# The paired mix products of a recurrent layer: a 32-column product of one of the two issued by itself ahead of the rest

## The chip, the core and the metric

The kernel runs on one core of a Trainium2 chip. The metric is the time of one execution on the device in microseconds (us). Three executions of the kernel before took 1084.72, 1081.46 and 1083.66 us; their median is 1083.66 us. A further execution was recorded by the hardware profiler, and all profile rows below are from that one.

A core has five engines, each with an instruction queue of its own that runs in order: PE (matrix products, with weight loads listed apart as PEld), DVE (vector), ACT (scalar functions), POOL (a second vector engine), and SP (which here only issues DMAs). Products land in PSUM, which has eight banks of 128 x 512 float32 values. DVE or ACT must read a bank out before it can be used again.

## The reference, cut to what matters

Four layers follow each other on an input `x` of 32 sequences, 64 positions, 256 features: a small attention layer (L0), two transformer layers with self-attention, cross-attention and an MLP (L1, L2), and a recurrent layer (L3). The change is in L3, whose head is this:

```python
xn = _ln(x, ln1_w, ln1_b)
sx = _token_shift(xn, state[:, i1])
xxx = jnp.tanh((xn + sx * maa_x) @ maa_w1).reshape(b, l, 5, 1, EXTRA_MAA)
xxx = jnp.matmul(xxx, maa_w2).reshape(b, l, 5, E)
x5 = xn[:, :, None] + sx[:, :, None] * (maa_stack + xxx)
...
k = (x5[:, :, 0] @ Wk.T).reshape(b, l, H, S)
v = (x5[:, :, 2] @ Wv.T).reshape(b, l, H, S)
```

So there are five mixes `x5[:, :, m]`, m = 0 to 4, each the product of a 32-wide piece of `xxx` with a 32 x 256 matrix, and each is then the input of one projection: 0 of the keys, 1 of the decay, 2 of the values, 3 of the receptance, 4 of the gate. After the projections a scan runs along the 64 positions, then come a group norm, an output projection and a feed-forward block. All in float32.

## The kernel before

**Tiling.** The 2048 rows of `x` (32 sequences times 64 positions) stay on the chip. The recurrent layer works through them in eight steps, n = 0 to 7, of four sequences (256 rows) each. `recurrent(n, ...)` returns three lists of pieces for a step: `first` (norm, mixes, projections, decay, gate), `second` (spreading the values by DMA, the scan, reading it with the receptance, the group norm, the output projection) and `third` (the feed-forward block). Data lie transposed: 256 features as two halves (c = 0, 1) of 128 partitions, 256 rows along the free dimension.

**The order of the work.** Each piece has a due time, and `emit` traces all pieces in the order of these times. Step n begins about one unit after step n - 1. Worked out from the parameters in lines 9 to 15 and the weights in lines 775 to 777, the norm of step n is due at n - 0.2, `mix(2, 3)` at n + 0.59, `mix(0, 1)` at n + 0.89 and `mix(4)` at n + 1.39; so the norm of step n + 1, due at n + 0.8, stands between the two paired mixes of step n. The pieces of the MLP of L2 that are left over (`late`) are interleaved with the steps in the same way. The final order within each engine's queue is not this one: a planner goes through the traced instructions with a simulated clock, and at each moment gives an engine the ready instruction that was traced earliest. An instruction that is the first to write a tile is ready only when one of the buffers of the tile's tag is free in that simulation. `tc.high_priority()` puts instructions ahead of all others that are ready, and `tc.issue_after(i)` keeps them behind `i` in their queue.

**PSUM.** The eight banks are shared out by tag (line 92): two each for `mm`, `sc` and `tp`, one each for `pc` and `pd`. In the recurrent layer `sc` has two kinds of users: the norm at the head of a step, `norm("x", ...)` in line 775, which takes one bank for its transposes (`pln_r`, line 163) and one for the token shift (`pst_r`, line 170), and the mixes (`px5_...`, which the profile lists as `px_r`).

**The mixes, lines 676 to 692.** `mix(*ms)` takes a bank for each mix in `ms` and lists four products for a pair, two for `mix(4)`: the stationary operand is a 32 x 128 piece of the matrix, the moving operand 32 x 256 of `ta` (or `tb` for m = 4), and the output one half c of the bank. Mix m uses partitions 32(m mod 4) to 32(m mod 4) + 31 of both operands, so the two mixes of a pair use different row groups of PE's array. The list runs c = 0: m = 3, m = 2; c = 1: m = 3, m = 2 (or 1, 0, 1, 0). `at_once` (lines 124 to 129) issues the first of them at its normal priority and the other three behind it with high priority. In the profile each float32 product is two weight loads and two matmul passes, so a pair of mixes shows as eight `MATMUL px_r` entries.

Then line 689 computes `(bank + maa_stack) * sx` on DVE, in two halves for each mix, which frees the bank, and line 692 adds `xn` on POOL. The projections `vals` (pv_r), `recept` (pr_r), `keys` (pk_r), `gate` (pg_r) and the decay (pdc_r, pw_r) follow, all on PE. DVE also runs the long operations of `second`: products with keys and receptance (line 782) and the scan (line 797), which read and write `vb_r`.

Of the kernel before, what the change touches and what calls it, by code (L numbers as in the profile page):

```python
# [23 lines left out]
P = 128  # L24
# [7 lines left out]
XM = 32  # L32
# [48 lines left out]
def tile_xattn_stack(ctx: ExitStack, tc: tile.TileContext, a: dict, out: bass.AP):  # L81
# [31 lines left out]
    def vec(name, i=0):  # L113
        c = VEC[name] + i
        return vecs[:, c : c + 1]
# [8 lines left out]
    def at_once(matmuls):  # L124

        first = matmuls[0]()
        with tc.issue_after(first.ins), tc.high_priority():
            for m in matmuls[1:]:
                m()

    def mm(ps, sta, mov, start=True, stop=True):
        return lambda: nc.tensor.matmul(ps, sta, mov, start=start, stop=stop)  # L132
# [467 lines left out]
    RB, RR = GB // 2, GR // 2  # L600

    def recurrent(n, pool, c3):
# [3 lines left out]
        st = {}  # L606
# [5 lines left out]
        def both(name, tag="mm"):  # L612

            return bank(name, tag).rearrange("p (c t) -> p c t", c=2)

        def tile_(name, bufs=2, shape=None, p=pool, tag=None):
            return p.tile(shape or [P, 2, RR], FP, tag=tag or name, name=f"{name}_{t}", bufs=bufs)
# [28 lines left out]
        def sx_(key, c):  # L646
            return st["d" + key][:, c].rearrange("p b t -> p (b t)")
# [28 lines left out]
        def mix(*ms):  # L676

            banks, mms = {m: both(f"px5_{t}_{m}", "sc") for m in ms}, []

            for c in range(2):  # L680
                for m in reversed(ms):
                    lw, rt = (c3["mw2a"], st["ta"]) if m < 4 else (c3["mw2b"], st["tb"])
                    part = slice((m % 4) * XM, (m % 4 + 1) * XM)
                    mms.append(mm(banks[m][:, c], lw[part, c * P : (c + 1) * P], rt[part, :RR]))
            at_once(mms)
            for m in ms:
                d = st["x5", m] = tile_(f"x5_{m}", tag="x5", bufs=3)
                for c in range(2):
                    nc.vector.scalar_tensor_tensor(  # L689
                        d[:, c], banks[m][:, c], vec("L3_maa_stack", 2 * m + c), sx_("x", c), ALU.add, ALU.mult  # L690
                    )
                nc.gpsimd.tensor_tensor(d, d, st["x"], ALU.add)  # L692
# [81 lines left out]

        first = [(0.5, lambda: norm("x", "L3_ln1_w", "L3_ln1_b", t, 1)), (0.0, first_mix), (1.2, maa)]
        first += [(0.85, lambda: mix(2, 3)), (1.7, vals), (0.85, lambda: mix(0, 1)), (1.7, recept), (1.7, keys)]
        first += [(0.85, lambda: mix(4)), (0.5, decay_a), (0.85, decay_b), (0.85, own_term), (1.7, gate)]


# [117 lines left out]
    wts, c3 = {}, {}  # L897
# [342 lines left out]
```

## Time and profile before

| what | value |
|---|---|
| three timed executions, median | 1083.66 us (1081.46 to 1084.72) |
| the profiled execution, its own time | 1080.68 us |
| its span, first to last instruction | 1078.9 us |
| PE busy | 983.6 us, 91% of the span, 10764 matmul passes |
| PEld busy | 787.8 us, 73% |
| DVE busy | 806.2 us, 75% |
| ACT busy | 549.2 us, 51% |
| POOL busy | 532.2 us, 49% |
| mean granted PE clock | 0.962 of full |

The span is the time from the first to the last instruction; the execution's own time is 1080.68 - 1078.9 = 1.78 us more than that. The busy time of an engine is the union of its instructions; matmuls overlap in a pipeline, so a full PE column does not mean that PE does as much as it could. A row of the timeline gives the start, the length, the engine, the line, the operation, output<-inputs, shapes and count, and in brackets how long the engine sat idle before it and what ended that. "L132" is the helper `mm`, through which the mixes and the over-keys sums go; the names `px_r` and `pa_r` tell them apart. The chain of waits goes back from the last instruction to whatever released it, so its rows say which engine's work set the end at each moment.

### The profile page before, as it was taken

What the parts mean: (1) busy time and instruction counts of PE and PEld (TensorE: products, weight loads), DVE (VectorE), ACT (ScalarE), POOL (GpSimd) and SP (SyncE); (2) the same over time, 40 slices, a digit from 0 to 9 for tenths busy, and PEclk for the clock granted to TensorE, in tenths of its full rate; (3) what the DMA queues carried; (4) which work ended last, traced back from release to release, by engine and by line L of the source; (5) the groups of instructions that cost most, each with busy time, mean ns of one, the idle gap of its engine ahead of it and who ended that gap; (6) DMA issues with size and microseconds to landing.
All of it is one profiled execution on the core that took longest, in us unless ns stands there. A gap on an engine that the chain in (4) does not pass through costs nothing.

```text
span 1078.9 us, 26319 instructions
## 1 busy us (share of the span) xinstructions
PE 983.6 (91%) x10764; PEld 787.8 (73%) x10764; DVE 806.2 (75%) x1513; ACT 549.2 (51%) x1271; POOL 532.2 (49%) x552
## 2 busy tenths in 40 slices
PE   8998999899989999989989999898989898988966
PEld 4886776667778989877767778787768677765645
DVE  5864688878877654777787887647887987999983
ACT  4743653554456644864454555454436464453334
POOL 4343766767657344756577665442434434153200
PEclk9999998999999999989899999999889999998889
DMA  9300111111100100140111101112122121332400
GB/s 301 105 21 21 23 45 32 38 25 27 26 22 7 40 1 21 46 138 22 41 39 28 26 21 32 31 36 66 41 70 60 50 61 40 95 76 69 98 11 29
DMA packets 45947, 53.39 MB, mean 49 GB/s; under 512 B 16146, under 2 KB 40068, under 8 KB 43780
## 3 DMA queue, kind: packets, MB, share of 16 engines
q1 hardware_dynamic: 40292, 49.60, 17.1%
q10 hardware_dynamic: 5536, 2.12, 0.8%
q8 instruction: 85, 1.39, 0.5%
q14 instruction: 34, 0.28, 0.1%
HBM read 38.83 MB, written 4.21 MB: 40 GB/s over the span
## 4 chain that ended last, share of the span: by engine, by line
PE 43%; DVE 32%; ACT 8%; POOL 8%; issue 4%; DMA 3%; SPq 0%; ACTq 0%; POOLq 0%; DVEq 0%
DVE vb_r L797 6%; PE pf_L1m L187 4%; PE pf_L2m L187 3%; DVE vb_r L782 3%; PE pfo_L1m L187 3%; POOL s_L2c L463 2%; DVE x L198 2%; POOL s_L1c L463 2%; PE pr L312 2%; PE pfo_L2m L187 2%; PE pwo_r L843 1%; PE px_r L132 1%; PE pq_L1c L187 1%; DVE s_L1c L458 1%; POOL s_L1s L463 1%
## 5 line engine op out<-in xcount | busy, mean ns | idle before, releaser
L692 POOL TENSOR_TENSOR x_r<-x_r,xn_r 128x512 f32<-128x512 f32 x40 | 63.6, 1604 | 113.7 <-DVE x_r L689 111.8
L797 DVE TENSOR_TENSOR_SCAN vb_r<-wsh,vb_r 128x512 f32<-128x512 f32 x64 | 77.6, 1276 | 5.6 <-ACT wsh L696 4.1
L463 POOL TENSOR_TENSOR s_L1s<-s_L1s,n 128x512 f32<-128x512 f32 x32 | 43.0, 1356 | 39.9 <-DVE s_L1s L458 39.2
L187 PE MATMUL pf_L2m<-lnT_L2m,w_L 128*128 128x256 f32 x384 | 57.8, 303 | 1.7 <-ACT vbd L430 0.7
L187 PEld LDWEIGHTS pf_L2m<-lnT_L2m,w_L 128*128 128x128 f32 x384 | 51.8, 202 | 7.6 <-issue 2.5
L187 PE MATMUL pfo_L2m<-w_L,hT_L2m 128*128 128x256 f32 x384 | 55.2, 291 | 1.5 <-DVE hT_L2m L581 1.5
L463 POOL TENSOR_TENSOR s_L2s<-s_L2s,n 128x512 f32<-128x512 f32 x32 | 43.0, 1360 | 26.9 <-DVE s_L2s L458 26.3
L187 PE MATMUL pfo_L1m<-w_L,hT_L1m 128*128 128x256 f32 x384 | 54.5, 288 | 1.6 <-POOL hT_L1m L580 0.8
L187 PE MATMUL pf_L1m<-lnT_L1m,w_L 128*128 128x256 f32 x384 | 51.9, 288 | 3.9 <-ACT hf_L1m L577 1.2
L463 POOL TENSOR_TENSOR s_L2c<-s_L2c,n_L2c 128x512 f32<-128x512 f32 x32 | 41.6, 1320 | 27.6 <-DVE s_L2c L458 26.7
L463 POOL TENSOR_TENSOR s_L1c<-s_L1c,n_L1c 128x512 f32<-128x512 f32 x32 | 41.3, 1309 | 25.8 <-DVE s_L1c L458 24.8
L187 PEld LDWEIGHTS pf_L1m<-lnT_L1m,w_L 128*128 128x128 f32 x384 | 47.5, 191 | 7.2 <-ACT hf_L1m L577 2.1
L187 PEld LDWEIGHTS pfo_L2m<-w_L,hT_L2m 128*128 128x128 f32 x384 | 48.7, 190 | 5.2 <-issue 2.7
L187 PEld LDWEIGHTS pfo_L1m<-w_L,hT_L1m 128*128 128x128 f32 x384 | 49.3, 191 | 3.4 <-POOL hT_L1m L580 1.0
L580 POOL TENSOR_SCALAR hT_L1m<-hf_L1m 128x512 fp32r<-128x512 f32 x32 | 21.8, 682 | 55.4 <-ACT hf_L1m L577 53.5
L577 ACT ACTIVATE hf_L1m<-pf_L1m,b_L 128x256 f32<-128x256 f32 x64 | 26.6, 471 | 42.3 <-PE pf_L1m L187 39.9
L581 DVE TENSOR_TENSOR hT_L1m<-hf_L1m,hT_L1m 128x512 fp32r<-128x512 f32 x32 | 25.3, 791 | 30.1 <-POOL hT_L1m L580 30.1
L581 DVE TENSOR_TENSOR hT_L2m<-hf_L2m,hT_L2m 128x512 fp32r<-128x512 f32 x32 | 24.7, 772 | 26.7 <-POOL hT_L2m L580 26.6
L580 POOL TENSOR_SCALAR hT_L2m<-hf_L2m 128x512 fp32r<-128x512 f32 x32 | 22.2, 694 | 40.1 <-ACT hf_L2m L577 39.8
L577 ACT ACTIVATE hf_L2m<-pf_L2m,b_L 128x256 f32<-128x256 f32 x64 | 26.6, 472 | 28.5 <-PE pf_L2m L187 23.0
L782 DVE TENSOR_TENSOR vb_r<-vb_r,ksh 128x2048 f32<-128x2048 f32 x16 | 38.3, 2409 | 2.7 <-DMA vb_r<-vd_r 2.7
L282 ACT ACTIVATE att<-pe,nmx 128x256 f32<-128x256 f32 x64 | 29.5, 476 | 19.3 <-DVE nmx L280 17.2
(388 smaller groups left out, 3062.1 us busy)
## 6 DMA issues: line engine op xcount, KB each, us to landing
vb_r<-vd_r SPq DMA_DIRECT2D x16, 1024.0 KB
raw_w_L<-in_L_w_dram SPq DMA_DIRECT2D x4, 1024.0 KB
y<-in_y_dram SPq DMA_DIRECT2D x8, 256.0 KB
x<-in_x_dram SPq DMA_DIRECT2D x8, 256.0 KB
ctxT_L1c<-in_yT_dram SPq DMA_DIRECT2D x4, 512.0 KB
kbd<-kT_L1s SPq DMA_DIRECT2D x64, 32.0 KB
kbd<-kT_L1c SPq DMA_DIRECT2D x64, 32.0 KB
kbd<-kT_L2s SPq DMA_DIRECT2D x64, 32.0 KB
```

The costliest lines, as they stand in the source:

```text
L132: return lambda: nc.tensor.matmul(ps, sta, mov, start=start, stop=stop)
L187: nc.tensor.matmul(ps, sta[x], mov[y], start=(at == 0), stop=(at == n - 1))
L198: nc.vector.tensor_tensor(xs, xs, ps, ALU.add)
L282: nc.scalar.activation(att[:, 2 * h + c, :], pe[:, c, :], AF.Exp, bias=nmx[:, h, c : c + 1], accum_out=rs[:, h, c : c + 1],)
L312: nc.tensor.matmul(pr[:, m, h, :], att[:, 2 * h + c, m * P : (m + 1) * P], xvT[:, c, h, :], start=(c == 0), stop=(c == 1),)
L463: nc.gpsimd.tensor_tensor(s[:, r], s[:, r], n(j).unsqueeze(1).broadcast_to([P, 8, S]), ALU.add)
L577: nc.scalar.activation(raw[:, i], ps[:, i], AF.Gelu_apprx_tanh, bias=w()["b1"][:, 2 * f2 + i : 2 * f2 + i + 1])
L580: nc.gpsimd.tensor_scalar(h[:, 0], raw, 1.0, 0.0, ALU.mult, ALU.add)
L581: nc.vector.tensor_tensor(h[:, 1], raw, h[:, 0], ALU.subtract)
L692: nc.gpsimd.tensor_tensor(d, d, st["x"], ALU.add)
L782: nc.vector.tensor_tensor(v, v, x.unsqueeze(1).broadcast_to([P, 4, 2 * RR]), ALU.mult)
L797: nc.vector.tensor_tensor_scan(v[:, d], flat(st["wsh"]), v[:, d], 0.0, ALU.mult, ALU.add)
```

## The change

For a pair of mixes, one more product is issued ahead of the four: half c = 0 of the pair's first mix (`ms[0]`: m = 2 or m = 0) for the first 32 of its 256 columns (`few = XM = 32`). It is issued at normal priority and is not part of the list given to `at_once`. It is the first to write that mix's bank. The list then holds the same four products in the same order, except that half 0 of `ms[0]` covers columns 32 to 255. For `mix(4)`, `few` is 0 and nothing changes. The products themselves are moved into a helper `add`.

```diff
@@ -677,11 +677,19 @@
             banks, mms = {m: both(f"px5_{t}_{m}", "sc") for m in ms}, []
 
+            def add(m, c, cols):
+                lw, rt = (c3["mw2a"], st["ta"]) if m < 4 else (c3["mw2b"], st["tb"])
+                part = slice((m % 4) * XM, (m % 4 + 1) * XM)
+                mms.append(mm(banks[m][:, c, cols], lw[part, c * P : (c + 1) * P], rt[part, cols]))
+
+
+            few = XM if len(ms) > 1 else 0
+            if few:
+                add(ms[0], 0, slice(0, few))
+                mms.pop()()
             for c in range(2):
                 for m in reversed(ms):
-                    lw, rt = (c3["mw2a"], st["ta"]) if m < 4 else (c3["mw2b"], st["tb"])
-                    part = slice((m % 4) * XM, (m % 4 + 1) * XM)
-                    mms.append(mm(banks[m][:, c], lw[part, c * P : (c + 1) * P], rt[part, :RR]))
+                    add(m, c, slice(few if c == 0 and m == ms[0] else 0, RR))
             at_once(mms)
```

## The prediction

> **What bounds the kernel now.** I begin with the page: the span, the busy times, and the chain of waits by engine.
>
> ```profile
> span 1078.9 us, 26319 instructions
> ...
> PE 983.6 (91%) x10764; PEld 787.8 (73%) x10764; DVE 806.2 (75%) x1513; ACT 549.2 (51%) x1271; POOL 532.2 (49%) x552
> ...
> PE 43%; DVE 32%; ACT 8%; POOL 8%; issue 4%; DMA 3%; SPq 0%; ACTq 0%; POOLq 0%; DVEq 0%
> ```
>
> PE is the busiest engine, but it holds only 43% of the chain and DVE holds 32%. The changed pieces run only in the last 366 us (first `px_r` at 713 us), so I read that stage next, as busy time in five stretches; the columns are the stretch, its length, and busy time (instructions) of PE, PEld, DVE, ACT, POOL, then PE clock, DMA share and GB/s.
>
> ```profile
> 700.00:780.00 80.00, 74.70 (x540) 63.09 (x539) 53.86 (x88) 40.50 (x85) 31.71 (x40) 0.94 0.20 48
> 780.00:860.00 80.00, 71.39 (x455) 56.20 (x456) 67.52 (x99) 36.64 (x72) 30.99 (x26) 0.94 0.25 60
> 860.00:940.00 80.00, 73.44 (x484) 59.87 (x483) 65.60 (x96) 42.12 (x86) 25.27 (x27) 0.98 0.22 54
> 940.00:1020.00 80.00, 72.04 (x395) 50.95 (x394) 78.05 (x109) 32.76 (x67) 31.20 (x23) 0.89 0.39 94
> ```
>
> PE is the fuller engine up to 780 us; from 940 us DVE leaves only 2 us in 80 free, and PE has 8 free. The chain agrees: up to 741 us it is almost all PE, later it lives on DVE's L797 scans and L782 products.
>
> Then I went through all 24 groups of `px_r` in PE's timeline: eight are `mix(4)`, untouched, and 16 are pairs. In 12 pairs the eight passes stand together; in four, all of `mix(0, 1)` (steps 2, 4, 5, 7), they come as four, something else, four. The first row is a pair together; the next four are one split pair and what follows it; the last three another.
>
> ```profile
> 713.14 1.13 PE L132 MATMUL px_r<-ta_r,mw2a 32*128 32x256 f32 x8
> ...
> 794.22 1.12 PE L132 MATMUL px_r<-ta_r,mw2a 32*128 32x256 f32 x4
> 795.27 0.66 PE L163 MATMUL pln_L2m<-ident,xn_L2m 128*128 128x128 f32 x4
> 795.86 1.13 PE L132 MATMUL px_r<-ta_r,mw2a 32*128 32x256 f32 x4
> 800.19 3.33 PE L192 MATMUL pr_r<-x_r,Wr 128*128 128x256 f32 x7 [3.21 <-DVE gt_r L773]
> ...
> 885.23 1.13 PE L132 MATMUL px_r<-ta_r,mw2a 32*128 32x256 f32 x4
> 886.28 1.13 PE L827 MATMUL pgv_r<-sq_r,avg 128*128 128x256 f32 x4
> 887.35 1.13 PE L132 MATMUL px_r<-ta_r,mw2a 32*128 32x256 f32 x4
> ```
>
> Eight passes of two row groups take 1.13 us, as long as four of one: the products of a pair that alternate cost PE half. A split costs one more block, 795.27 - 794.22 = 1.05 us.
>
> **Part 1, what goes: the second block of a split pair.** If every pair alternates, PE loses one block in each of four: 1.05 us three times, and 994.82 - 993.33 = 1.49 us in step 7, where the granted clock was 0.57. Together 4.6 us of PE time. What is it worth to the end? Each place by its rows:
> - Step 2 (794 to 797): PE is done by 796.99 and then idles 3.21 us for DVE, and DVE takes up the mix (L689) only at 803.16, after a scan, L833, L773 and L782. Worth nothing.
> - Step 4 (885 to 888): the chain of waits names both blocks, but DVE runs a scan from 887.96 to 892.52 that doesn't read them, and L689 starts at 892.44 as that ends. Worth 0 to 0.6 us; I take 0, because the next row that needs the mix stood behind the scan.
> - Step 5 (939.70 to 943): `pa_r` between the blocks waits for DVE's L782, and `pwo_r` behind them for DVE's L834 at 942.91. Worth nothing.
> - Step 7 (993 to 998): DVE has scans from 993.11 to 1004.34 and reaches this mix at 1008.02. Worth nothing.
>
> So the saved work hides behind DVE. What is late next in each place is already late: DVE's scan queue.
>
> **Part 2, what comes: 16 short products**, each two weight loads (32 x 128) and two passes of 32 columns. The trace has no such product, so bounds. *Passes*: from below the over-lapped small ones of L666, 16 in 712.00 - 711.64 = 0.36 us, 0.023 each; from above the transposes `pln_r`, four in 0.60 us, 0.15 each; I take `pst_r` in between, eight in 1.06 us, 0.133 each, as its weights are 128 columns wide too: 0.27 for two. *Entering and leaving the 32-row layout*: four solo passes of `mix(4)` occupy PE for 1.06 us (725.64 to 726.70), where four of eight full-height passes take 1.73/2 = 0.865 us, so 0.20 us.
> - Standing alone (the four split pairs): 0.27 + 0.20 = 0.47 us, bounds 0.25 and 0.50.
> - Directly ahead of its pair (the other 12, where both banks were free when the first product was issued): no further change of layout; its row group gets two passes more, and its half 0 loses 2 x 32 columns, 64/256 x 0.216 = 0.05 us. 0.27 - 0.05 = 0.21 us, bounds 0 (the other row group hides it) and 0.50 (something comes between).
>
> The Trainium skill, TensorEngine Tiling, Key Properties, says that a change of the tiling mode drains TensorE, which speaks against a short product by itself. The 0.20 us is what the trace shows of that; PEld's "issue" gaps at `px_r` (4.2 us in 12) point the same way. The same skill, TensorE: Matmul & The Clock Gate, LDWEIGHTS, counts a weight load by its columns, 128/1.2 = 107 ns, so that by an estimate from this page the two short passes would be 0.21 us whatever their rows, and the sum below lower by 0.2 us.
>
> PE in all: 12 x 0.21 + 4 x 0.47 - 4.6 - 4 x 0.05 = -0.4 us; from -3.8 (12 x 0 + 4 x 0.25 - 4.6 - 0.2) to +3.4 (12 x 0.50 + 4 x 0.50 - 4.6).
>
> On the path, only the pairs that the chain holds whole:
>
> ```profile
> 713.21 1.06 PE px_r L132 x8
> ...
> 721.30 1.07 PE px_r L132 x8
> ...
> 737.58 1.06 PE px_r L132 x8
> ```
>
> Three x 0.21 = +0.6 us (0 to 1.5). The other nine lie beside DVE, a DMA or ACT on the chain (at 749.00, for instance, PE idles 0.96 us soon after); if that cover were gone, they would cost 9 x 0.21 = 1.9 us more.
>
> **Part 3, what moves: who gets the second bank.** Before, the first product took the bank that came free first, and the claim on the second ran with high priority. Now the short product takes the first at normal priority, and the claim on the second is `at_once`'s first product, at normal priority too. Between the two, PE may be given anything that is ready and was traced earlier. No DMA is issued by these lines; the DMAs of `maa`, `vals` and `spread` move only as their inputs do, on SP's queue. The row that shows who waits for a late mix:
>
> ```profile
> POOL x_r L692 <- DVE x_r L689: 111.8, 23, 12.0
> ```
>
> POOL waits for L689 111.8 us in total, up to 12.0: the mixes reach their projections late because of DVE, not of PE. DVE gets both halves of a split pair later than now (m = 1 was ready a block early); cost bounded by 0 and one block, 1.05 us; I take 0, since in all four places L689 started 0.4 us or more after the second block had ended (943.42 - 943.03 in step 5).
>
> **Sum**: 1080.68 + 0.6 - 0 = 1081.3 us for the profiled execution. That execution lay 2.98 us under the median of the runs; on the median it is 1083.66 + 0.6 = 1084.3. I say 1084 us.
>
> **Rivals.**
> 1. *The path as summed* (forecast), 1084 us, own range 1081 to 1087. For it: every split pair stands beside a full DVE. Chance 0.36.
> 2. *Slower: the next step's norm takes the second bank.* Place: `mix(0, 1)`. The norm of step n + 1 is traced earlier and uses the same two banks; the second claim of a mix has lost its high priority. If the short product holds one bank while the norm's transposes and its token shift go one after the other through the other bank, the mix waits from `pln_r` to the end of `sx_r`: 720.21 - 717.64 = 2.57 us at the least, 792.26 - 786.80 = 5.46 when ACT is late; and L689 can then fall behind a scan of 4.57 us. Against it: in the four splits the norm is already through. It decides from two steps on the chain: +5 to +11, with one in between 1089 us. Any other reordering of DVE by the planner that puts one more scan ahead of L689 costs the same 4.57. Chance 0.31.
> 3. *Faster: PE is the bound more than the chain says.* PE is over 89% full to 1020 us; if the low bound of its time is all on the path, -3.8, and one mix gets ahead of a scan (-4.57 at best), 1075 to 1080; 1079 us. Against it: the idle rows above. Chance 0.27.
> 4. *It doesn't do what it says*: something still comes between and pairs stay split, so only the 16 short products are added: 0.6 + a block or two, 1086 us. Chance 0.06.
>
> **The numbers.** One measurement of this kernel can tell about 0.3% (3.3 us) from no change; that is 1080.4 to 1086.9. Case 1 gives 0.28 within, 0.05 slower, 0.03 faster; case 2 0.30 slower, 0.01 within; case 3 0.25 faster, 0.02 within; case 4 half and half. Faster 0.28, within 0.34, slower 0.38. Cases of both signs hold much of the chance, so the range reaches into both: 1077 to 1093 us.
>
> **What would show it.** Right: 16 pairs of eight full passes together, PE busy within 4 us of 983.6, L689 of steps 2, 4, 5, 7 where it was, behind the scans; the chain through steps 0 and 1 longer by a few tenths. Part 2 wrong: PE rows of the short products far from 0.2 to 0.5 us. Case 2: `pln_r` or `pst_r` between a short product and its pair, and longer POOL waits for L689. Case 3: fewer PE idle rows from 780 us on. Wrong altogether: a different order of scans and mixes on DVE, which no sum over rows foresees.

## The result, and the profile after

The changed kernel took 1089.07 us (median of eight runs, 1085.28 to 1091.72), the kernel before 1082.80 us (median of eight, 1080.00 to 1087.76): a ratio of 1.006 with a 95% interval from 1.0035 to 1.0085, so it is slower by 0.6%. The profiled execution took 1089.28 us. All line numbers behind the change have moved by 8: L689 is now L697, L692 is L700, L696 is L704, L765 is L773, L782 is L790 and L797 is L805.

The page of the changed kernel, with the three lines that were read before:

```profile
span 1087.4 us, 26395 instructions
...
PE 986.3 (91%) x10796; PEld 792.5 (73%) x10796; DVE 808.0 (74%) x1513; ACT 549.8 (51%) x1271; POOL 526.8 (48%) x552
...
PE 40%; DVE 35%; POOL 8%; ACT 7%; issue 4%; DMA 4%; SPq 2%; ACTq 0%; DVEq 0%; POOLq 0%
```

The span is 8.5 us longer; PE, DVE and ACT are each busy for less than 3 us longer, the weight loads (PEld) for 4.7 us longer, and POOL for less. Most of the time went into waiting. The share of PE in the chain has fallen and that of DVE has risen. The busy time by stretches of the changed kernel (the columns are those shown for the kernel before):

```profile
700.00:780.00 80.00, 73.62 (x565) 61.44 (x565) 53.27 (x98) 35.81 (x76) 31.26 (x44) 0.91 0.17 41
780.00:860.00 80.00, 69.58 (x463) 54.01 (x465) 66.58 (x89) 40.31 (x78) 29.98 (x25) 0.93 0.22 54
860.00:940.00 80.00, 75.19 (x507) 62.71 (x500) 62.16 (x101) 37.25 (x78) 25.93 (x30) 0.95 0.25 61
940.00:1020.00 80.00, 68.56 (x411) 49.32 (x410) 78.27 (x104) 38.15 (x76) 25.44 (x21) 0.96 0.35 84
```

Up to 860 us PE, the fullest engine there, is busy for 74.70 - 73.62 + 71.39 - 69.58 = 2.9 us less than before. DVE is again full in the last stretch. These stretches count from the start of the span, and the changed kernel comes to its first `px_r` 4.0 us later, so the table only hints that something in the first steps of the recurrent layer is late; the count from the first `px_r`, below, shows it.

**What the change set out to do has happened.** All 16 pairs now alternate. PE's timeline of the changed kernel shows the two forms:

```profile
717.12 1.30 PE L132 MATMUL px_r<-ta_r,mw2a 32*128 32x32 f32 x10
...
753.48 0.40 PE L132 MATMUL px_r<-ta_r,mw2a 32*128 32x32 f32 x2
753.81 0.65 PE L163 MATMUL pln_L2m<-ident,xn_L2m 128*128 128x128 f32 x4
756.05 1.93 PE L132 MATMUL pa_r<-vb_r,sel 128*32 128x256 f32 x16 [1.58 <-DVE vb_r L790]
757.90 2.07 PE L132 MATMUL px_r<-ta_r,mw2a 32*128 32x256 f32 x8
```

In 11 pairs the short product stands directly ahead of its pair: ten passes in 1.30 us, where eight took 1.13, so it costs 0.17 us. In five it stands apart, and the eight passes behind follow each other: in four of them other work comes between, and in step 7 PE only waits 0.32 us for L697 to free the second bank. Apart, the next product starts 753.81 - 753.48 = 0.33 us after it. That isn't the whole price. Taken pass by pass around the short product at 845.28, it is 0.31 us from the start of the last pass of 128 rows ahead of it (844.97) to its own, and 0.32 us from the first such pass behind it (845.61) to the next (845.93); otherwise these passes follow each other every 0.22 us. That is 0.10 us more at each end, so a short product by itself costs 0.33 + 0.20 = 0.53 us; around the one at 945.59 the same sum comes out. The chain of waits of the changed kernel still holds three such pairs whole, each 0.17 us longer than before (1.23 for 1.06):

```profile
717.19 1.23 PE px_r L132 x9
...
725.46 1.23 PE px_r L132 x9
...
741.90 1.23 PE px_r L132 x9
```

That is 0.5 us in all, far from 6 us. What else differs is the order of the work: from the first `mix(0, 1)` on, the planner wrote other queues. Compared by instruction (the short products left aside), 575 positions of PE's queue hold something else, 188 of DVE's, 117 of ACT's, 10 of POOL's and none of SP's. The first 713 us are in the same order in both kernels.

**How to compare profiles here.** The first `px_r` came at 713.14 us in the profile of before and at 717.12 us in that of after, although the work up to there is in the same order. Over all the profiles below this moment lies between 713.14 and 719.73 us. I count from the first `px_r` of each kernel, and so leave that spread out. Before needed 365.8 us from there to the end of the span and after 370.3 us; to the first scan of step 1 it was 68.3 and 71.8, so most of the difference is there after one step.

### The profile page after: what moved, and what is told of

It is laid out like the page before. It is cut to its first block, busy times and chain, and to the rows that moved or that the text cites. A ratio compares the mean times of both kernels' runs of the same rounds, so it can differ in the third digit from the quotient of the medians.

```text
span 1087.4 us, 26395 instructions
## 1 busy us (share of the span) xinstructions
PE 986.3 (91%) x10796; PEld 792.5 (73%) x10796; DVE 808.0 (74%) x1513; ACT 549.8 (51%) x1271; POOL 526.8 (48%) x552
## 4 chain that ended last, share of the span: by engine, by line
PE 40%; DVE 35%; POOL 8%; ACT 7%; issue 4%; DMA 4%; SPq 2%; ACTq 0%; DVEq 0%; POOLq 0%
DVE vb_r L805 6%; DVE vb_r L790 4%; PE pf_L1m L187 4%; PE pf_L2m L187 3%; PE pfo_L1m L187 3%; POOL s_L2c L463 2%; DVE x L198 2%; PE pfo_L2m L187 2%; POOL s_L1c L463 2%; DVE x_r L697 2%; POOL s_L1s L463 1%; PE pr L312 1%; SPq L403 1%; PE pq_L2c L187 1%; DVE s_L1c L458 1%
## 5 line engine op out<-in xcount | busy, mean ns | idle before, releaser
L700 POOL TENSOR_TENSOR x_r<-x_r,xn_r 128x512 f32<-128x512 f32 x40 | 62.9, 1587 | 132.1 <-DVE x_r L697 128.3
L805 DVE TENSOR_TENSOR_SCAN vb_r<-wsh,vb_r 128x512 f32<-128x512 f32 x64 | 77.3, 1267 | 10.2 <-ACT wsh L704 9.4
L790 DVE TENSOR_TENSOR vb_r<-vb_r,rT_r 128x2048 f32<-128x2048 f32 x16 | 39.2, 2449 | 0.0
L790 DVE TENSOR_TENSOR vb_r<-vb_r,ksh 128x2048 f32<-128x2048 f32 x16 | 37.8, 2378 | 1.6 <-DMA vb_r<-vd_r 1.6
```

The lines of the kernel that those rows point to most:

```text
L790: nc.vector.tensor_tensor(v, v, x.unsqueeze(1).broadcast_to([P, 4, 2 * RR]), ALU.mult)
L805: nc.vector.tensor_tensor_scan(v[:, d], flat(st["wsh"]), v[:, d], 0.0, ALU.mult, ALU.add)
```

## The experiments

In the runs that hold an order, the queues of PE, DVE, ACT and POOL are written out from about the first instruction that differs. Each instruction is chained to the one ahead of it on its engine, for the order alone; no wait is added. This addition is the same in all of them and is shown once; the lists themselves (`ORDER`) are left out, and each order is told in words:

```diff
+def pin(nc, tc):
+    traced = nc.cur_bb.bb.instructions
+    for order in ORDER:
+        for k, j in zip(order, order[1:]):
+            tc.add_manual_dep(
+                traced[j], traced[k].name,
+                mybir.DependencyInfo(mybir.DependencyClass.NoSync, mybir.DependencyReason.DATA), reason="pin",
+            )
...
         tile_xattn_stack(tc, aps, out)
+        pin(nc, tc)
```

The table gives all runs, of 6 to 12 executions each. Each was timed beside executions of the kernel before on the same chip, and its ratio is to those (their medians lie between 1081.73 and 1084.48 us), not to the first row; so it is not the quotient of two medians of this table. The last two columns are from one profiled execution each: us from the first `px_r` to the first scan of step 1, and to the end of the span. The profiled executions of "no short products, new order" (1094.87 us) and of "old order, `xn_r` first" (1090.74 us) are at the slow end of their kernels, so their last column is high.

| kernel | median, us | ratio (95% interval) | to scan of step 1 | to the end |
|---|---|---|---|---|
| before | 1082.80 | 1 | 68.3 | 365.8 |
| changed | 1089.07 | 1.006 (1.0035 to 1.0085) | 71.8 | 370.3 |
| short products, old order | 1082.49 | 0.9995 (0.9975 to 1.0016) | 66.4 | 364.7 |
| no short products, new order | 1089.70 | 1.0059 (1.0040 to 1.0078) | 72.3 | 373.3 |
| old order up to step 2, then new | 1080.87 | 0.9989 (0.9965 to 1.0013) | 66.3 | 363.7 |
| new order up to step 2, then old | 1088.81 | 1.0061 (1.0037 to 1.0084) | 72.5 | 371.6 |
| short product for `mix(2, 3)` alone | 1083.96 | 1.0010 (0.9986 to 1.0033) | 66.6 | 367.3 |
| short product for `mix(0, 1)` alone | 1085.68 | 1.0033 (1.0012 to 1.0053) | 68.2 | 368.8 |
| short product of 64 columns | 1096.79 | 1.0126 (1.0085 to 1.0168) | 72.4 | 380.5 |
| the same, old order | 1082.75 | 1.0015 (0.9995 to 1.0034) | 66.1 | 364.3 |
| second claim at high priority | 1110.07 | 1.0240 (1.0205 to 1.0275) | 68.5 | 390.9 |
| new order, decay chain earlier | 1086.01 | 1.0030 (1.0008 to 1.0052) | 70.9 | 370.6 |
| new order, `hf_L2m` first on ACT | 1082.52 | 1.0013 (0.9991 to 1.0035) | 69.3 | 367.0 |
| old order, `xn_r` first on ACT | 1086.21 | 1.0020 (0.9992 to 1.0048) | 71.5 | 370.8 |

### The order against the products

Theory: the order costs, the products don't. Rival: the products, or the bank that the short one holds, cost. The first kernel has the changed kernel's instructions in before's order: 12 short products directly ahead of their pairs, and where a pair was split, the short product in the place of the first block and the whole pair in that of the second.

> All instructions of the changed kernel, but with every engine's queue held to the order of the kernel before: the 16 short products are added, 12 directly ahead of their pair, 4 (where a pair was split) in the place of the first block, with the whole pair in the place of the second. Theory A (the time came with the new order of the queues that the planner wrote; the short products themselves cost their few tenths on the path): within 0.2% of the kernel before, 1083 to 1084.5 us, since the sum of the prediction was +0.6. Rival B (the extra passes on a PE that is 91% full): as slow as the changed kernel, 1088 to 1090 us.

The second has before's instructions, without any short product, in the order of the changed kernel.

> All instructions of the kernel before, no short product, but with every engine's queue held to the order of the changed kernel (half 0 of the pair's first mix is whole again). Theory A: as slow as the changed kernel or up to 1 us better, 1087 to 1089 us. Rival B: as the kernel before, 1082 to 1084 us.

Ratio 0.9995 with the products and without the new order, 1.0059 with the new order and without the products. The new order makes the whole loss; the products and the four pairs made whole together make no difference that the runs can tell (0.2% to either side). The rival is out. Nor is the granted clock the cause: over the timed runs of "new order up to step 2, then old" (next section) it is 0.963 in the mean, as in the runs of the kernel before beside it, and its ratio is 1.0061.

### Which part of the order

Both kernels have the short products. One follows before's order up to the second scan of step 2 (the instructions up to there on every queue) and the changed kernel's after it; the other the reverse.

> The changed kernel with its 16 short products; every engine's queue is held to the order of the kernel before up to the scan of step 2, e = 1 (the short products placed as in short_in_old_order), and to the order of the changed kernel from there on. Theory A1 (the loss is in steps 0 to 2, where the scans of steps 1 and 2 wait 5.3 us more for the decay than before): ratio to before within 0.3% of 1.000, so 1081 to 1087 us. Rival A2 (the loss is spread over all reordered steps): about half of it stays, 1.003, 1087 us; if it is all in the tail, 1.006.

> The other half: the changed kernel's own order up to the scan of step 2, e = 1, then the order of the kernel before. Theory A1: ratio 1.004 to 1.008, 1088 to 1093 us. Rival A2: about 1.003.

0.9989 against 1.0061: as far as the runs can tell, all of the loss comes with the order of steps 0 to 2. These two also tell of the wait that the prediction put forward, POOL's for L689 (L697). The rows are the columns engine, line, what it waited for: total, times, longest; first the changed kernel, then the old head with the new tail, then the new head with the old tail:

```profile
POOL x_r L700 <- DVE x_r L697: 128.3, 21, 13.0
```

```profile
POOL x_r L700 <- DVE x_r L697: 130.9, 23, 13.0
```

```profile
POOL x_r L700 <- DVE x_r L697: 102.4, 22, 15.6
```

It rose from 111.8 to 128.3 us with the change, but of these three the kernel with the longest waits in total is as fast as before, and the one with the shortest is slow. It is not what costs.

### One pair alone, and another size

```diff
-            few = XM if len(ms) > 1 else 0
+            few = XM if ms == (2, 3) else 0
```

> The change for mix(2, 3) alone, order left to the planner: eight short products, all beside pairs that were together before; mix(0, 1) as before. Nothing is to be gained here, so part 2 of the prediction alone gives +0.2 to +0.7 us. Theory A: it also gets an order of its own, so anything from 1079 to 1090 us. Rival B: half of the loss, about +3 us, 1086 us.

```diff
-            few = XM if len(ms) > 1 else 0
+            few = XM if ms == (0, 1) else 0
```

> The change for mix(0, 1) alone, order left to the planner: the pairs that were split are all here, so the change does its whole purpose with eight short products. By the path as summed it is worth nothing (0 to -0.6 us), so what is measured is the order that the planner writes: 1079 to 1095 us. If saved PE time counted, it would be the best of all variants, 1078 to 1081 us.

```diff
-            few = XM if len(ms) > 1 else 0
+            few = 64 if len(ms) > 1 else 0
```

> The change with a short product of 64 columns in place of 32, order left to the planner: on the chip the same work but for 32 columns, in the planner's clock a slightly longer first product, and an order that differs from the changed kernel's in 128 places on PE. If the time hangs on the order that the planner happens to write, it need not be that of the changed kernel: 1079 to 1095 us. If it hangs on the mechanism of holding a bank or on the short products, 1.005 to 1.008 as with 32 columns.

> The kernel of short_64_columns with every queue held to the order of the kernel before, as in short_in_old_order. If its 1.0126 came with the order alone, the ratio is 0.998 to 1.002 (1081 to 1085 us); if 64 columns cost anything by themselves, it stays above 1.005.

The planner is free in the first three. With `mix(2, 3)` alone the time is that of before, with `mix(0, 1)` alone 0.3% over it, with 64 columns 1.3%, and 64 columns in the old order are back at 1.0015 (0.9995 to 1.0034). A wider product costs nothing by itself either; each edit gets an order of its own. They don't lose in one place: `mix(0, 1)` alone comes to the scan of step 1 in 68.2 us, as before, and loses in the last steps: from the first `px_r`, it is 0.4 us behind before at the second scan of step 5, 5.4 us at the first of step 6 and 3.0 us at the end.

### The second claim

The line that issues the short product by itself is taken out, so that it heads the list of `at_once`: the short product runs at normal priority and all four others, the claim on the second bank among them, at high priority.

```diff
             if few:
                 add(ms[0], 0, slice(0, few))
-                mms.pop()()
```

> The short product stays, but heads the list that is given to at_once, so that the claim on the second bank has high priority again as in the kernel before. If the normal priority of that claim was the cause (rival C, the prediction's case 2), the time goes back to 1081 to 1085 us. Theory A: another order, and no reason for it to be better or worse, 1079 to 1092. Rival B: 1088 to 1090, since the short products are all still there.

1.024, the slowest of all. So the loss can't be put down to the lost priority of the second claim: giving it back produced an order that is far worse: in its profile the end comes 25.1 us later after the first `px_r` than in before, and 17.0 of them are lost behind the scans of step 5. What costs there I have not taken apart further.

### The decay chain

DVE's timeline of the changed kernel at the first scan of step 1, and that of the kernel before:

```profile
783.63 2.29 DVE L790 TENSOR_TENSOR vb_r<-vb_r,ksh 128x2048 f32<-128x2048 f32 x1 [1.59 <-DMA vb_r<-vd_r]
788.96 4.57 DVE L805 TENSOR_TENSOR_SCAN vb_r<-wsh,vb_r 128x512 f32<-128x512 f32 x4 [3.03 <-ACT wsh L704]
```

```profile
778.72 2.29 DVE L782 TENSOR_TENSOR vb_r<-vb_r,ksh 128x2048 f32<-128x2048 f32 x1 [2.75 <-DMA vb_r<-vd_r]
781.40 4.57 DVE L797 TENSOR_TENSOR_SCAN vb_r<-wsh,vb_r 128x512 f32<-128x512 f32 x4 [0.39 <-ACT vb_r L787]
```

The scan now waits 3.03 us for the decay (`wsh`), and that of step 2 waits 3.23 us for it where it waited 0.90. My first theory was that this wait is the loss. In step 1 `pw_r` is moved on PE ahead of 17 passes of `pfo_L2m` and `dT_r` on ACT ahead of the norm of L2; in step 2 the exponentials and `wsh` on ACT ahead of two norms.

> The changed kernel in its own order, with the decay chain alone moved up in two steps. Step 1: the two pw_r products on PE to directly behind pma_r, ahead of 17 pfo passes; the two tanh of the decay on ACT ahead of the norm of the next MLP half. Step 2: the two exponentials, wsh and the start-state copies on ACT ahead of that norm and of the feed-forward norm's copy. Theory A1: the two scans start about 2.2 and 1.6 us earlier, and if nothing else takes that back the ratio falls from 1.006 to about 1.0025 (1085 to 1088 us). Rival A2: these two waits are covered by others, and the ratio stays at 1.005 to 1.007.

DVE's row in that kernel:

```profile
785.36 4.57 DVE L805 TENSOR_TENSOR_SCAN vb_r<-wsh,vb_r 128x512 f32<-128x512 f32 x4 [0.86 <-ACT wsh L704]
```

The wait has shrunk from 3.03 to 0.86 us, but the scan came only 0.9 us sooner after the first `px_r` (70.9 for 71.8; 2.2 were expected), and the end of this profile is no earlier (370.6 for 370.3). The timed runs say something else: 1086.01 us and a ratio of 1.0030 are what theory A1 gave, but the interval (1.0008 to 1.0052) overlaps with that of the changed kernel and reaches into the rival's 1.005 to 1.007. So the times allow that the late decay costs up to half of the loss, and don't settle it. By the rows it isn't the whole: the wait on the decay was the last of several late inputs. The values' DMA was late as well: DVE's product of step 1, which waits for it, began 66.5 us after the first `px_r` in the changed kernel, 65.6 in before and 63.5 in the old order with the short products.

### One swap on ACT

So I went back along both inputs to the first thing that is late. The keys (`pk_r`) of step 1 begin 55.0 us after the first `px_r` in the changed kernel, 53.8 in before, 51.8 in the old order with the short products. PE's timeline of the changed kernel there:

```profile
763.57 3.03 PE L187 MATMUL pf_L2m<-lnT_L2m,w_L 128*128 128x256 f32 x12
...
767.58 1.70 PE L187 MATMUL pf_L2m<-lnT_L2m,w_L 128*128 128x256 f32 x12
772.10 2.71 PE L192 MATMUL pk_r<-x_r,Wk 128*128 128x256 f32 x8 [2.82 <-ACT hf_L2m L577]
774.74 1.94 PE L132 MATMUL pa_r<-vb_r,sel 128*32 128x256 f32 x16
```

PE, the fullest engine of this stretch, idles 2.82 us, for an activation of L2's MLP that reads out a bank. Behind it stand the keys and `pa_r`, which frees the values' buffer for the next DMA. ACT's timeline of the changed kernel says why the activation is late:

```profile
764.17 0.59 ACT L737 COPY rT_r<-pr_r 128x512 f32<-128x512 f32 x1 [4.31 <-PE pr_r L192]
768.71 1.10 ACT L155 ACTIVATE xn_r<-x,nmr_r,rstd_r 128x256 f32<-128x256 f32 x2 [3.96 <-DVE nmr_r L152]
769.82 1.28 ACT L577 ACT_TABLE_LOAD   x1
771.12 1.57 ACT L577 ACTIVATE hf_L2m<-pf_L2m,b_L 128x256 f32<-128x256 f32 x4
```

The same place in the kernel before:

```profile
764.71 1.28 ACT L577 ACT_TABLE_LOAD   x1 [4.31 <-PE pf_L2m L187]
766.00 0.84 ACT L577 ACTIVATE hf_L2m<-pf_L2m,b_L 128x256 f32<-128x256 f32 x2
766.73 1.09 ACT L155 ACTIVATE xn_r<-x,nmr_r,rstd_r 128x256 f32<-128x256 f32 x2
767.72 0.82 ACT L577 ACTIVATE hf_L2m<-pf_L2m,b_L 128x256 f32<-128x256 f32 x2
```

Two pairs of instructions have changed places. In the new order ACT takes up the norm `xn_r` first. That one needs `nmr_r` from DVE, and DVE's timeline of the changed kernel has a scan ahead of it:

```profile
762.45 6.18 DVE L805 TENSOR_TENSOR_SCAN vb_r<-wsh,vb_r 128x512 f32<-128x512 f32 x4
768.55 0.13 DVE L152 SCALAR_TENSOR_TENSOR nmr_r<-mv_r,rstd_r 128x2 f32<-128x2 f32 x1
```

So ACT stands 3.96 us behind a scan of another engine. The first product for `hf_L2m` had ended at 763.57 + 3.03 = 766.60 us, but the activation stands behind ACT's head and starts at 771.12. In before ACT waits for that product alone, runs two activations, and then the norm. The chain of waits of the changed kernel runs through these rows, from the scan over the norm and the activation to the keys (start, length, what):

```profile
762.53 6.10 DVE vb_r L805 x4
...
768.71 1.10 ACT xn_r L155 x2
...
771.12 0.85 ACT hf_L2m L577 x2
...
772.10 2.71 PE pk_r L192 x8
```

The test is that swap by itself, once undone in the new order and once made in the old one, in the lists of ACT alone (by the traced names):

```diff
- rT_r1  xn_r3_1  xn_r3_1  hf_L2m20_0  hf_L2m20_0  hf_L2m20_1
+ rT_r1  hf_L2m20_0  hf_L2m20_0  xn_r3_1  xn_r3_1  hf_L2m20_1
```

> The changed kernel in its own order with one swap: in step 1 ACT runs the first two activations of the MLP (hf_L2m, L577) ahead of the two of the norm (xn_r, L155), as before's order has them; every other queue is untouched. Theory A (ACT stands behind a scan: xn_r waits for DVE's nmr_r, which stands behind the scan of step 0; hf_L2m, though its product is ready, waits behind it, and so do the keys on PE, the sums over keys that free the values' buffer, the DMA into it and the decay): from the first px_r to the first scan of step 1 takes about 3 us less than the 71.8 us of the changed kernel, 68 to 69, and the time is about 1086 us, ratio 1.003. Theory B (the loss is in the late decay chain itself or in the products L652 behind the scan of step 2): no change, 71 to 72 us to the first scan of step 1, about 1089 us, ratio 1.006.

ACT's and then PE's timeline of this kernel:

```profile
763.34 0.84 ACT L577 ACTIVATE hf_L2m<-pf_L2m,b_L 128x256 f32<-128x256 f32 x2
765.80 1.09 ACT L155 ACTIVATE xn_r<-x,nmr_r,rstd_r 128x256 f32<-128x256 f32 x2 [1.62 <-DVE nmr_r L152]
766.80 0.81 ACT L577 ACTIVATE hf_L2m<-pf_L2m,b_L 128x256 f32<-128x256 f32 x2
```

```profile
762.95 1.70 PE L187 MATMUL pf_L2m<-lnT_L2m,w_L 128*128 128x256 f32 x12
764.49 1.89 PE L192 MATMUL pk_r<-x_r,Wk 128*128 128x256 f32 x8
768.09 1.07 PE L132 MATMUL pa_r<-vb_r,sel 128*32 128x256 f32 x16 [1.72 <-DVE vb_r L790]
```

All queues but ACT's are in the changed kernel's order. PE's wait ahead of the keys is gone, and the keys start 764.49 - 713.83 = 50.7 us after the first `px_r` instead of 55.0. The scan of step 1 comes after 69.3 us instead of 71.8, the end after 367.0 instead of 370.3. The ratio is 1.0013, and its interval (0.9991 to 1.0035) ends where that of the changed kernel (1.0035 to 1.0085) begins. The chain of waits no longer goes through `xn_r` and `hf_L2m` here. By the two ratios this one swap takes back 0.5 of the 0.6%, more than the half that was expected; that it takes back some is shown, that it is most of the loss is the estimate.

The wait has a second price that its length doesn't show: the clock that PE is granted behind it. In the changed kernel it is 0.66 of full from 772 to 777 us, and the same eight passes of `pk_r` take 2.71 us; with `hf_L2m` first it is 1.00 (764.4 to 770 us), and they take 1.89. In each of the six kernels here that run `xn_r` first, the trace has the clock at 0.50 for 3.4 to 6.8 us somewhere between 52.8 and 60.2 us after the first `px_r`; none of the other eight has that in this place.

> The kernel before in its own order with the same swap the other way round: in step 1 ACT runs the two activations of the norm (xn_r, L155) ahead of the first two of the MLP (hf_L2m, L577). No short products, every other queue untouched. Theory A: ACT waits about 4 us for nmr_r behind the scan, the keys come about 3 us later on PE, the first scan of step 1 begins about 70 to 72 us after the first px_r (68.3 in the profile of before, 66.3 in three runs in that order), and the time is about 1086 us, ratio 1.003 (up to 1.004). Theory B: no change, 66 to 68 us, about 1083 us, ratio 1.000.

ACT's and PE's timeline of the old order with the swap the other way:

```profile
769.17 1.09 ACT L155 ACTIVATE xn_r<-x,nmr_r,rstd_r 128x256 f32<-128x256 f32 x2 [4.00 <-DVE nmr_r L152]
770.26 1.28 ACT L577 ACT_TABLE_LOAD   x1
771.56 1.57 ACT L577 ACTIVATE hf_L2m<-pf_L2m,b_L 128x256 f32<-128x256 f32 x4
```

```profile
772.54 3.75 PE L192 MATMUL pk_r<-x_r,Wk 128*128 128x256 f32 x8 [3.83 <-ACT hf_L2m L577]
```

The same waits appear, 4.00 us on ACT as in the changed kernel and 3.83 on PE (2.82 there), with the granted clock at 0.50 behind them (772.5 to 778 us); the scan of step 1 comes after 71.5 us, the end after 370.8. One thing besides the swap differs: POOL's list begins behind this place, and one add of L692 runs ahead of the `hT_L2m` that follows the activation, where before has it behind. In the timed runs the median is 1086.21 for 1082.92, but they spread from 1077.63 to 1091.18, and the ratio of 1.002 has an interval (0.9992 to 1.0048) that holds no change as well. By the rows the swap makes the delay of the keys; by the times its size in this direction is not settled.

## Why the prediction was right in its range and wrong in its path, step by step

The forecast was 1084 us, no change that can be told; measured were 1089.07 us and +0.6%. The time lies in the range (1077 to 1093), at the place of rival 2, and slower had the largest of the three chances (0.38); but the case that was called the likeliest did not come. The range was that wide for the sake of rivals 2 and 3; that it holds a time with another cause is luck.

**Part 1, the second block of a split pair: right.** All pairs alternate, and the 4.6 us of PE time are worth nothing that can be told: in the old order the four pairs made whole and the 16 short products together give 0.9995. This fits the reasoning (DVE is late there anyway).

**Part 2, the short products: right in kind and nearly in size.** Ahead of the pair 0.17 us were measured for 0.21; by itself 0.53 for 0.47, a little over its upper bound of 0.50: 0.33 for the passes (0.27 in the sum), and at the two ends 0.20, as in the sum. On the chain 3 x 0.17 = 0.5 us for 0.6. PE is busy 986.3 us, within the 4 us given, though the sum of -0.4 was not exact: +2.7; the kernel without short products in the new order has 988.7, so this column moves by more than the products do. The Trainium skill, TensorEngine Tiling (Array Packing), Key Properties, says that a change of the tiling mode drains TensorE; the 0.10 us at each end would be the place for that, and no run here shows that they are a drain.

**Part 3, who gets the second bank: this step failed.** It said that PE may be given anything that is ready between the short product and its pair, priced only the norm and one more scan on DVE (as rival 2), and put the whole part at 0 in the sum. Measured were about 6 us, and they come with the new order. Something did come between in four pairs (in step 1 the transposes of L2's norm and the sums `pa_r`, four and 16 passes), but the cost did not arise there: the kernel with short products for `mix(2, 3)` alone has its pair of `mix(0, 1)` split around the same work, and it loses nothing that can be told. What was not priced is that the planner gives out all queues by a simulated clock, and that later choices on every engine can move with one insertion. The choice that, by the swap, cost the most was on ACT, an engine that the diff doesn't touch and whose order the prediction did not look at. Why the simulated clock put the norm first there is not shown.

**Rival 2 (1089 us)** has the time and not the mechanism. `pln_r` and `pst_r` did not come between a short product and its pair; "one more scan ahead of L689" is not what happened; and POOL's wait for L689, its witness, does not go with the time. That its sum comes to the measured time is luck. What is alike is only that something stood behind a scan: not L689 on DVE, but a norm on ACT, and behind it the activation on which PE waited. **Rival 3** is out: the PE time was saved in the old order too, and nothing faster than before came of it that can be told. **Rival 4** is out: pairs alternate.

"Wrong altogether: a different order of scans and mixes on DVE, which no sum over rows foresees" was the right kind of warning. It named DVE; the swap that was tested is on ACT.

**What stays open.** In the kernel with the swap undone, the scan of step 1 still waits 3.61 us for the decay and comes 69.3 us after the first `px_r`, where old orders need 66.1 to 68.3. Its chain of waits there runs over the 17 passes of `pfo_L2m`, `pw_r` and the decay, which is what the experiment on the decay chain had moved; undoing the swap and moving the decay chain together was not tried. In the profile of that experiment the granted clock was 0.50 for 6.8 us behind the late keys, and 3.4 us in that of the changed kernel, which may have hidden part of its gain. A further piece is in step 2. DVE's timeline of the changed kernel, then of the kernel before:

```profile
833.68 4.57 DVE L805 TENSOR_TENSOR_SCAN vb_r<-wsh,vb_r 128x512 f32<-128x512 f32 x4 [3.23 <-ACT wsh L704]
838.17 1.63 DVE L697 SCALAR_TENSOR_TENSOR x_r<-px_r,vecs,sx_r 128x256 f32<-128x256 f32 x4
839.72 2.41 DVE L652 SCALAR_TENSOR_TENSOR xk_r<-sx_fr,vecs,xn_fr 128x256 f32<-128x256 f32 x2
842.05 0.87 DVE L652 SCALAR_TENSOR_TENSOR xr_r<-sx_fr,vecs,xn_fr 128x256 f32<-128x256 f32 x2
```

```profile
825.44 0.88 DVE L652 SCALAR_TENSOR_TENSOR xk_r<-sx_fr,vecs,xn_fr 128x256 f32<-128x256 f32 x2 [1.74 <-POOL sx_fr L636]
826.24 0.88 DVE L652 SCALAR_TENSOR_TENSOR xr_r<-sx_fr,vecs,xn_fr 128x256 f32<-128x256 f32 x2
828.01 4.57 DVE L797 TENSOR_TENSOR_SCAN vb_r<-wsh,vb_r 128x512 f32<-128x512 f32 x4 [0.90 <-ACT wsh L696]
```

The L652 pairs, which filled time ahead of the scan, come behind it: from one scan of step 2 to the next it is 848.90 - 833.68 = 15.22 us, and was 840.61 - 828.01 = 12.60. But the stretch ahead of it, from the second scan of step 1 to the first of step 2, has become shorter by the work that left it, 32.0 us for 33.9. So the move costs 2.6 - 1.9 = 0.7 us, which the 2.41 us of `xk_r` (1.5 us more than before) would account for. This was not tried by itself.

## What to carry to other kernels

Where a planner writes the queues, price an inserted instruction in two sums: its own cost, and that of another order, which here were nothing that could be told (0.2% to either side) and 0.6%, and between 0.1% and 2.4% for neighbours of the same edit. Pin the old order around the new instructions before blaming them: one run tells the two sums apart. Where an order is worse, look for the in-order engine whose head waits for something behind a long operation of another engine while ready work stands behind it, and go back along the late inputs to the first of them; the wait that ends last may be only one of several that are late alike.

## What the runs showed of the hardware

- **DVE and POOL hold each other up.** The pair `xk_r` took 2.41 us in the changed kernel and 0.88 in before. POOL's timeline of the changed kernel, and of the kernel before:

```profile
839.16 2.68 POOL L700 TENSOR_TENSOR x_r<-x_r,xn_r 128x512 f32<-128x512 f32 x2 [4.25 <-DVE x_r L697]
```

```profile
833.50 4.58 POOL L692 TENSOR_TENSOR x_r<-x_r,xn_r 128x512 f32<-128x512 f32 x2 [8.09 <-DVE x_r L689]
```

Taken one by one, the two `xk_r` of the changed kernel end at 840.71 and 842.12, each 0.28 us after one of POOL's two adds (840.43 and 841.84). In before it is POOL that loses: its second add, 1.27 us elsewhere, lasts from 834.73 to 838.07, until 1.14 us after a product of DVE on two SBUF inputs (L782, 834.65 to 836.93). L689, which reads PSUM, kept its 0.47 us beside POOL. This agrees with the Trainium skill, SBUF — State Buffer, "Who interferes with whom": a DVE instruction with two SBUF inputs contends with a GpSimd (POOL) instruction that reads SBUF, over a shared pair of ports that is an exclusive lock.
- **The same work takes different times.** Up to the first `px_r`, in one order in all kernels here, the profiles took 713.14 to 719.73 us, a spread of 6.6 us. That is as large as the effect of the change, so single profiles were compared from that point on.
